# A hybrid of state-space scan, attention and routed experts on one core: the tail of the last image re-ordered

## The chip, the cores and the metric

The kernel runs on one core of a Trainium2 chip. The metric is device time in microseconds for one execution over four images. A core has TensorE (PE; its weight loads are listed as PEld), VectorE (DVE), ScalarE (ACT), GpSimd (POOL) and SyncE (SP). Each has its own queue and works through it in order. An engine waits when what stands at the head of its queue needs a result of another engine or of a transfer. Most transfers are issued from SP; the indirect ones, which scatter or gather rows by a list of places, from POOL.

## The reference, cut to what matters

The input x is 4 images of 384 channels by 32 by 32 positions, that is 1024 tokens per image.

```
# layer 0
x = x + gelu(layernorm(four-direction selective scan of groupnorm(x)))
# layer 1, on tokens t of width 384
t = t + softmax_causal(ln(t) Wq (ln(t) Wk)^T / sqrt(384)) ln(t) Wv
s = softmax(ln(t) gate_w + gate_b)             # 4 experts
keep the 2 largest of s per token, divide them by their sum + 1e-9
t = t + sum over the 2 kept e of s[e] * (gelu(ln(t) w1[e] + b1[e]) w2[e] + b2[e])
```

The selective scan of layer 0 runs over 1024 positions in four directions, for 384 channels with 16 states each. A hidden layer of an expert is 1536 wide. All is float32.

## The kernel before, in words

**Scan and ticks.** The scan is cut into 768 units (NU), 192 per image, each a 128 by 1024 tile. A loop over a counter called `clock` emits the program: in each tick it emits one unit of the scan (L192 decay, L648 input, L654 scan, L671 product, L696 row sums), and then as much other work as fits. The other work is written as Python generators. A generator yields ("pe", n) after n microseconds' worth of TensorE work, ("wait", k) to be taken up k ticks later, or ("inner", 0) to be taken up inside the next tick. `go_on` (L1837) hands out a budget per tick, `pace[0]`: 4.4 in attention (PACE_A), 3.1 elsewhere (PACE_E). Side generators get up to 1.0 each, and the first generator in `waiting` gets what is left. `defer(k, f)` puts an action k ticks later: mostly the copy that empties an accumulator. None of this is time on the chip; it only fixes the order in each engine's queue. From tick 772 (NU + 4) on there are no more scan units: what is emitted then is the tail.

**Buffers.** TensorE writes into banks of the accumulator memory. Four are free for side work in the scan; in the tail four more come (y_end and v_end, two halves each), eight in all. `banks.take` takes the one that has been free longest. Eight `slots` in on-chip memory are shared by weight tiles, blocks of rows and their results.

**The last image's layer.** After the scan of image b, `finish` does its layernorm (`layernorm`, L726): mean products (L739), subtraction (L747), squares on ACT, variance products (L766), square root on ACT, reciprocal (L779), products that spread the result over partitions (L785), multiplication (L795); then GELU on ACT, a load of x (xr, L971) and the addition (L979). `attention` follows: `scaled_tokens` does a second norm in the same manner (var_at L1000, L1011, L1015, L1020, L1036), then query products (pq, L1068), value products (pv, L1079), and for each of eight blocks of 128 tokens: scores (L1098), softmax on DVE and ACT, transposition (L1141), values (L1165, L1169), statistics (L1177). For images 0 to 2 this runs under the scan of the next image; for image 3 (`alone`) nothing is left to run under.

**Routing.** `ready` (L1220) routes the tokens in three groups, blocks 0 to 3, 4 and 5, 6 and 7: normalise, transpose (pxt, L1248), gate products (L1265), softmax with an exponential on ACT (L1284 to L1296), a comparison that counts the larger scores (L1297 to L1307), running counts (L1309), products that turn counts into places (L1324 to L1337), kept shares (mk, L1343 to L1347), places (L1355 to L1370), a transposition of mk (pm, L1376), and two scatters per block into xsd (L1385), which is in order of expert. After group 2, `table` (L1411) computes for each of NBLK = 11 blocks of 256 rows its expert, its place, and how many rows it holds.

**Experts.** `experts` (L1458) does the eleven blocks: load rows (xg, L1521), transpose (L1530), first product (ph, L1591) with GELU on ACT, second product (py, L1636), copy to yt (one half on DVE, L1650, one on ACT, L1652), store to ysd (L1654). Weight tiles are loaded (L1497) as slots come free. For the last image, six tiles go at a time, and a block computes 256, 128 or no rows, by its count: TensorE reads all eleven counts into registers (L1558) before the first block, and VectorE sets every accumulator to zero first (L1584, L1627), so that what isn't computed is zero.

**Combination.** For each block i of 128 tokens: gather the two expert rows of every token (L1682), load the token rows t2 and the gates (L1689, L1690), multiply identities by the shares on ACT, and sum on TensorE t2, b2 and the two choices (`add_up`, L1708); copy (L1715) and store (L1716). For image 2 this is `combine` and `joined`, which fall into the tail, around the last image's norms. For image 3, `early` is started when block 9 has been stored: first gathers, loads, and sums of all but the second choice; `late`, after block 10, gathers the second choice and ends the sums. The store of block 10 writes the tensor that the first gathers read, so it waits for them:

```
elif j == NBLK - 1:
    side.append((late if alone else combine)(b))
```

Of the kernel before, what the change touches and what calls it, by code (L numbers as in the profile page):

```python
# [9 lines left out]
F32 = mybir.dt.float32  # L10
# [7 lines left out]
P = 128  # L18
# [29 lines left out]
PACE_E = 3.1  # L48
BT = 256
# [6 lines left out]
def hybrid_kernel(  # L56
# [669 lines left out]
    def layernorm(dst, src, name, lag):  # L726
# [55 lines left out]
        for h in range(n):  # L782
# [8 lines left out]
            yield "pe", 1.0  # L791
        yield "inner", 0
# [193 lines left out]
    def scaled_tokens(b, yb):  # L986
# [19 lines left out]
        slots.give(*[f"sq_at_{b}_{c}" for c in range(M)])  # L1006
        rs = one.tile([P, NH, P], F32, tag=f"rs{NH}", name=f"rs_at_{b}")
# [212 lines left out]
    def ready(b, h, yb, rows, moments):  # L1220
# [42 lines left out]
        for q in range(n):  # L1263
            for c in range(M):
                nc.tensor.matmul(  # L1265
                    pg[:, q * E : (q + 1) * E], xts[q][:, c * P : (c + 1) * P], gw[:, c, :],
                    start=(c == 0), stop=(c == M - 1),
                )
        yield "pe", 0.65 * n
# [10 lines left out]
        def over(v):  # L1280
# [3 lines left out]
        nc.vector.tensor_reduce(red, sc, AX.X, ALU.max)  # L1284
        nc.vector.tensor_tensor(sc, sc, over(red), ALU.subtract)
        act(sc, sc, AF.Exp)

        cmp = [
            one.tile([P, 4, E, E], F32, tag=f"cmp{i}", name=f"cmp{i}_{name}")[:, :n] for i in range(2)
        ]  # L1290
        each = sc.unsqueeze(3).to_broadcast([P, n, E, E])
        other = sc.unsqueeze(2).to_broadcast([P, n, E, E])
        yield "wait", 1
        nc.vector.tensor_reduce(red, sc, AX.X, ALU.add)
        nc.vector.reciprocal(red, red)
        nc.vector.tensor_tensor(sc, sc, over(red), ALU.mult)  # L1296
        nc.vector.tensor_tensor(cmp[0], other, each, ALU.is_gt)  # L1297
        nc.vector.tensor_tensor(cmp[1], other, each, ALU.is_ge)
        nc.vector.tensor_tensor(
            cmp[1], cmp[1], lower.unsqueeze(1).to_broadcast([P, n, E, E]), ALU.mult  # L1300
        )
        nc.vector.tensor_tensor(cmp[0], cmp[0], cmp[1], ALU.max)
        cnt = small("cnt", name, n, E)
        nc.vector.tensor_reduce(cnt, cmp[0], AX.X, ALU.add)

        sel = small("sel", name, E, n)
        nc.vector.tensor_single_scalar(sel.rearrange("p e q -> p q e"), cnt, 1.5, ALU.is_lt)  # L1307
        cum = counts[b, h] = sm.tile([P, E, n], F32, tag=f"cum{h}", name=f"cum_{name}")
        nc.vector.tensor_tensor_scan(  # L1309
            cum.rearrange("p e q -> p (e q)"), fresh[n].rearrange("p e q -> p (e q)"),  # L1310
            sel.rearrange("p e q -> p (e q)"), 0.0, op0=ALU.mult, op1=ALU.add,
        )
# [22 lines left out]
        if h == LAST:  # L1335
            for i in range(LAST + 1):
# [3 lines left out]
                )  # L1340
        yield "pe", 1.5
        mk = small("mk", name, n, E)
        nc.vector.scalar_tensor_tensor(mk, cnt, 1.5, sc, ALU.is_lt, ALU.mult)  # L1343
        nc.vector.tensor_reduce(red, mk, AX.X, ALU.add)
        nc.vector.tensor_scalar_add(red, red, 1e-9)
        nc.vector.reciprocal(red, red)
        nc.vector.tensor_tensor(mk, mk, over(red), ALU.mult)  # L1347
# [25 lines left out]
        banks.give(f"place_{name}")  # L1373
        pm = yield from banks.take(f"pm_{name}")
# [7 lines left out]
        placed = places[b]  # L1382
        for q in range(n):
            for i in range(2):
                nc.gpsimd.indirect_dma_start(  # L1385
                    out=views[2 * (q0 + q) + i],
                    out_offset=bass.IndirectOffsetOnAxis(
                        ap=placed[:, q0 + q, i : i + 1], axis=0
                    ),
                    in_=rows[:, q, :], in_offset=None,  # L1390
                )
# [562 lines left out]
```

## Time and profile before

| | |
|---|---|
| Median of 3 runs | 3745.76 us (3745.48 to 3747.65) |
| Profiled execution | 3738.39 us |
| Its span, first to last instruction | 3736.7 us |
| Mean granted TensorE clock | 0.859 |
| PE busy | 2996.1 us (80%) |
| DVE busy | 3020.3 us (81%) |
| ACT busy | 2061.5 us (55%) |
| POOL busy | 1980.5 us (53%) |
| Moved by DMA | 798.42 MB, 214 GB/s over the span |

The last scan instruction ends at 3158.0 us, so the tail is 579 us long. A busy share is an average over the scan, where VectorE is at work nearly all the time, and the tail, where TensorE is. In the lines shown below, "out<-in" names what an instruction writes and reads, L and a number give its line, and the arrow in a line on waiting points to the engine, or the transfer, whose work came last.

### The profile page before, as it was taken

How to read it: one execution, taken by the hardware profiler on the slowest of the kernel's cores; microseconds unless marked ns; L12 is line 12 of the kernel's file. 1: busy time of each engine (PE TensorE's matmuls, PEld its weight loads, DVE VectorE, ACT ScalarE, POOL GpSimd, SP SyncE). 2: the span in 40 equal slices, each digit the busy share in tenths (PEclk: the TensorE clock that was granted, in tenths of full speed). 3: DMA queues.
4: the chain of work that ended last, by engine and by line, in shares of the span. 5: the costliest groups of instructions: out<-in, count | busy, mean ns of one | idle time of the engine just before them, and what ended most of it. 6: DMA issues, size and time to landing. Idle time of an engine off the chain costs nothing. (4 is left out here: it accounts for less than half of the span.)

```text
span 3736.7 us, 41646 instructions
## 1 busy us (share of the span) xinstructions
PE 2996.1 (80%) x13267; PEld 1798.4 (48%) x13267; DVE 3020.3 (81%) x2417; ACT 2061.5 (55%) x3268; POOL 1980.5 (53%) x931
## 2 busy tenths in 40 slices
PE   4566755678589899779569999779589999778997
PEld 1233423334346566344345665344256665556775
DVE  6999888899989999998999999999989998131110
ACT  5778787556466566456546665356356564342121
POOL 2677667645656555764656555765666666010001
PEclk7677777779789999769779999879689999888998
DMA  6658644543577888554567888553378876215555
GB/s 198 216 201 291 241 179 186 201 166 135 195 243 277 293 300 297 198 196 153 177 224 277 292 286 292 193 206 129 123 253 301 294 279 207 76 47 180 180 187 178
DMA packets 405202, 798.42 MB, mean 214 GB/s; under 512 B 47500, under 2 KB 278620, under 8 KB 404972
## 3 DMA queue, kind: packets, MB, share of 16 engines
q1 hardware_dynamic: 390572, 770.01, 59.3%
q0 software_dynamic: 8192, 25.17, 2.1%
q8 instruction: 117, 1.92, 0.2%
q10 hardware_dynamic: 6208, 0.39, 0.1%
q14 instruction: 113, 0.93, 0.1%
HBM read 680.44 MB, written 115.02 MB: 213 GB/s over the span
## 5 line engine op out<-in xcount | busy, mean ns | idle before, releaser
L671 POOL TENSOR_TENSOR h<-h,bc 128x1024 f32<-128x1024 f32 x768 | 1818.4, 2372 | 1208.9 <-DVE v L648 1031.8
L654 DVE TENSOR_TENSOR_SCAN h<-da,v 128x1024 f32<-128x1024 f32 x768 | 1749.3, 2283 | 80.7 <-PE v L958 40.8
L192 ACT ACTIVATE da<-dt,a 128x1024 f32<-128x1024 f32 x768 | 884.7, 1162 | 774.8 <-DVE h L654 636.7
L648 DVE TENSOR_TENSOR v<-du,bc 128x1024 f32<-128x1024 f32 x664 | 851.4, 1282 | 95.9 <-PE y L696 26.2
L696 PE MATMUL y<-h,sel 128*32 128x512 f32 x3072 | 560.0, 703 | 186.2 <-POOL h L671 178.6
L1591 PE MATMUL ph<-turned,w 128*128 128x256 f32 (+1 forms) x2772 | 631.1, 384 | 45.4 <-DMA w<-in_w 32.2
L1636 PE MATMUL py<-w,ht 128*128 128x384 f32 x1776 | 606.2, 493 | 11.3 <-DMA w<-in_w 11.3
L1591 PEld LDWEIGHTS ph<-turned,w 128*128 128x128 f32 x2772 | 523.4, 193 | 164.2 <-issue 51.1
L1636 PEld LDWEIGHTS py<-w,ht 128*128 128x128 f32 x1776 | 335.2, 192 | 277.7 <-issue 40.0
L192 ACT ACTIVATE ht<-ph,b1t 128x256 f32<-128x256 f32 x470 | 196.7, 471 | 330.6 <-PE ph L1591 329.8
L696 PEld LDWEIGHTS y<-h,sel 128*32 128x32 f32 x3072 | 104.4, 120 | 507.7 <-POOL h L671 290.6
L1682 POOL DMA_INDIRECT g<-ysd,places x64 | 83.4, 1303 | 369.6 <-DMA g<-gtd 329.8
L958 PE MATMUL v<-ident,st 128*128 128x128 f32 x832 | 156.5, 351 | 117.4 <-DVE h L654 113.0
L192 ACT ACTIVATE st<-turn,bt 128x128 f32<-128x128 f32 x832 | 245.4, 564 | 0.1
L958 PEld LDWEIGHTS v<-ident,st 128*128 128x128 f32 x832 | 127.7, 183 | 164.0 <-DVE h L654 94.6
L182 ACT ACT_TABLE_LOAD x122 | 156.5, 1283 | 12.2 <-issue 10.1
L510 PE MATMUL pdt<-xd,wdt 12*128 12x512 f32 x184 | 117.2, 774 | 23.5 <-ACT st L192 7.2
L1385 POOL DMA_INDIRECT xsd<-fx,places x32 | 36.3, 1135 | 153.6 <-DVE places L1370 145.8
L1169 PE MATMUL po<-vt,pt 128*128 128x384 f32 x242 | 91.6, 528 | 9.0 <-ACT pt L1059 9.0
L1098 PE MATMUL ss<-axn,qt 128*128 128x512 f32 (+3 forms) x252 | 91.8, 508 | 5.6 <-ACT pr L192 4.5
L192 ACT ACTIVATE dt<-pdt,dtb 128x512 f32<-128x512 f32 x96 | 64.6, 690 | 49.4 <-PE pdt L510 48.1
L192 ACT ACTIVATE ht<-ht 128x3072 f32<-128x3072 f32 x33 | 91.3, 2766 | 0.4
(381 smaller groups left out, 2656.1 us busy)
## 6 DMA issues: line engine op xcount, KB each, us to landing
w<-in_w SPq DMA_DIRECT2D x528, 384.0 KB
bc<-rows SPq DMA_DIRECT2D x384, 512.0 KB
dt<-dts SPq DMA_DIRECT2D x192, 512.0 KB
du<-dts SPq DMA_DIRECT2D x192, 512.0 KB
dts<-dt SPq DMA_DIRECT2D x48, 512.0 KB
dts<-du SPq DMA_DIRECT2D x48, 512.0 KB
xg<-xsd SPq DMA_DIRECT2D x44, 384.0 KB
ysd<-yt SPq DMA_DIRECT2D x44, 384.0 KB
```

Of the source, the lines that this page charges most:

```text
L182: nc.scalar.preload_act_table_set(kind)
L192: return nc.scalar.activation(dst, src, f, **more)
L510: nc.tensor.matmul(pss[i], wdt[r, m * P : (m + 1) * P], xd[r, bass.ts(h, 512)], start=True, stop=True,)
L648: return nc.vector.tensor_tensor(u["v"], spread["du4", n], spread["bc", n][:, 0, :], ALU.mult)
L654: nc.vector.tensor_tensor_scan(u["h"][:, ::step], u["da"][:, ::step], u["v"][:, ::step], 0.0, op0=ALU.mult, op1=ALU.add,)
L671: product = units[n]["product"] = nc.gpsimd.tensor_tensor(h, h, spread["bc", n][:, 1, :], ALU.mult)
L696: units[n]["row"] = nc.tensor.matmul(y, sel, h, start=first, stop=last, tile_position=(0, jj * DJ))
L958: nc.tensor.transpose(u["v"][:, t * P : (t + 1) * P], st[:, t, u["j"] * P : (u["j"] + 1) * P], ident)
L1098: nc.tensor.matmul(ps[:, : e - o], qt[:, c, i * P : (i + 1) * P], xn[o // 512][:, c, : e - o], start=(c == 0), stop=(c == M - 1 and (alone ...
L1169: nc.tensor.matmul(po[:, :C], pts[i][:, j, :], vt[:, j, :], start=False, stop=(j == i))
L1591: nc.tensor.matmul(ps[:, i * BT : i * BT + n], t[:, c, i * P : (i + 1) * P], xt[:, c, :n], start=(c == 0), stop=(c == M - 1),)
L1636: nc.tensor.matmul(pss[i][:, :C], hts[j][:, 2 * c + f, i * P : (i + 1) * P], tiles["2", j, c][0][:, f, :], start=(c == 0 and f == 0), stop ...
```

## The change

It does the following.

- **Finer steps.** From tick NU + 4 on the pace is 1.5 (PACE_T) in place of 4.4 or 3.1.
- **The third image's sums between the last image's norms.** `combine` is replaced for image 2 by `held_back`. It loads and gathers at the end of the scan into tiles that the scan leaves (not slots), and puts the eight sums on a list. `fill_in` takes from it: three sums after the spreading products of the last image's layernorm, two after the variance products of `scaled_tokens`, the remaining three after the gate products of group 2.
- **Experts by raw scores.** For the last image the comparison reads the scores, not the probabilities, which have the same order. The exponential, the probabilities and the kept shares come later: the scatters no longer stand behind the transposition of mk.
- **Registers and loads ahead.** TensorE reads the eleven counts when the first load of rows has been emitted, ahead of the transposes. Expert 0 is given at least one block, so that the first block's expert and place are known constants, in all images. Four weight tiles of the last image are loaded before routing ends.
- **Zeroing.** VectorE's zeroing is gone. Where a block has 128 rows or none, TensorE writes an identity over the rest, as a transpose: finite values, in rows that belong to no token and that no later step uses. This adds one branch.
- **The end.** t2 and gates of the last image are loaded when block 2 has been stored. The first choice is added to t2 by VectorE (`add_choice`); TensorE sums t2 and b2 of all eight blocks in eight banks (`sum_up`), and then only the second choice. The last block's copies are both on ACT.

The diff, cut to its core:

```diff
+PACE_T = 1.5
+PART = 2.6
...
             backs.append(spread_)
             yield "pe", 1.0
+        if name == f"l0_{B - 1}":
+            fill_in(3)
...
         slots.give(*[f"sq_at_{b}_{c}" for c in range(M)])
+        if b == B - 1:
+            fill_in(2)
...
+        if h == LAST:
+            gated.add((b, h))
...
+        if not alone:
+            exponents()
+            yield "wait", 1
+            probabilities()
+        cum = choice()
...
+        if alone:
+            exponents()
         yield "pe", 1.5
+        if not alone:
+            kept()
...
+        if alone:
+            yield "wait", 1
+            for q in range(n):
+                scatter(q)
+            routed.add((b, h))
+            probabilities()
+            kept()
+            yield "wait", 1
...
+        nc.vector.tensor_scalar_max(n, n, 1.0)
...
         def look_up(j):
+            if j == 0:
+                expert[j] = block[j] = 0
...
+        def by_rows(j, run, fill):
             with tc.If(filled[j] > P) as whole:
                 run(BT)
             with whole.Else():
-                with tc.If(filled[j] > 0):
+                fill(P)
+                with tc.If(filled[j] > 0) as some:
                     run(P)
+                with some.Else():
+                    fill(0)
...
-                    if alone:
-                        nc.vector.memset(ps, 0.0)
...
+                def fill(o):
+                    for f, t, w, name, ps in parts:
+                        for i in range(2):
+                            nc.tensor.transpose(
+                                ps[:, i * BT + o : i * BT + o + P], ident, ident
+                            )
...
-                        if alone:
-                            nc.vector.memset(pss[i][:, :C], 0.0)
...
+                def fill(o):
+                    if c0 == 0:
+                        for m in range(M):
+                            nc.tensor.transpose(pss[o // P][:, bass.ts(m, P)], ident, ident)
...
-                    if alone and i == 1:
+                    if alone and i == 1 and j < NBLK - 1:
...
-                if alone and j == NBLK - 2:
-                    side.append(early(b))
+                if alone and j == 2:
+                    side.append(beside_all(b))
+                elif alone and j == NBLK - 2:
+                    side.append(first_choice(b))
                 elif j == NBLK - 1:
-                    side.append((late if alone else combine)(b))
+                    side.append((late if alone else combine if b < B - 2 else held_back)(b))
...
+        while alone and fetched[0] < 4:
+            while not slots.ready():
+                yield "wait", 1
+            weights()
         while (b, LAST) not in routed:
             yield "wait", 1
         yield from load(0)
+        for j in range(NBLK if alone else 0):
+            count_rows(j)
...
+    def beside_all(b):
+        for i in range(L // P):
+            g = dtp.tile([P, L], F32, tag=("dt4", "du4")[i // 4], name=f"g_{b}_{i}")
+            z = (hp if i < 7 else dap).tile(
+                [P, L], F32, tag="h" if i < 7 else "da", name=f"z_{b}_{i}"
+            )
+            closing[b, i] = g, z
+            nc.sync.dma_start(z[:, :C], t2_d[b][bass.ts(i, P), :])
+            nc.sync.dma_start(g[:E, 2 * C : 2 * C + P], gates_d[b][:, bass.ts(i, P)])
+            for k in range(2) if b < B - 1 else (1,):
+                act(z[:, 2 * C + k * P : 2 * C + (k + 1) * P], ident, AF.Copy,
+                    scale=shares[b][:, i, k : k + 1])
+            yield "wait", 1
...
+    def held_back(b):
+        while clock[0] < NU:
+            yield "wait", 1
+        side.append(beside_all(b))
+        for i in range(L // P):
+            while (b, i) not in closing:
+                yield "wait", 1
+            g, z = closing[b, i]
+            for k in range(2):
+                gather(b, i, g, k)
+            ready_sums.append((b, i))
+            yield "wait", 1
+        while (B - 1, LAST) not in gated:
+            yield "wait", 1
+        while ready_sums:
+            fill_in(1)
+            yield "pe", 2.4
+
+    def fill_in(n):
+        for _ in range(min(n, len(ready_sums))):
+            b, i = ready_sums.pop(0)
+            g, z = closing[b, i]
+            ps = banks.now(f"pz_{b}_{i}")
+            add_up(ps, g, z, ("t2", "b2", 0, 1), True, True)
+            def put(b=b, i=i, ps=ps, z=z):
+                put_out(b, i, ps, z)
+                banks.give(f"pz_{b}_{i}")
+            defer(1, put)
+
+    def first_choice(b):
+        for i in range(L // P):
+            gather(b, i, closing[b, i][0], 0)
+        yield "wait", 2
+        for i in range(L // P):
+            add_choice(b, i, 0)
...
     def late(b):
...
+            gather(b, i, closing[b, i][0], 1)
+        pss = {}
         for i in range(L // P):
-            while len(closing[i]) < 3:
-                yield "wait", 1
-            g, z, ps = closing[i]
-            add_up(ps, g, z, (1,), False, True)
-            put_out(b, i, ps, z)
+            pss[i] = yield from banks.take(f"pz_{b}_{i}")
+            sum_up(b, i, pss[i], False)
+        for i in range(L // P):
+            g, z = closing[b, i]
+            for m in range(M):
+                nc.tensor.matmul(
+                    pss[i][:, bass.ts(m, P)], g[:, C + m * P : C + (m + 1) * P],
+                    z[:, 2 * C + P : 2 * C + 2 * P], start=False, stop=(m == M - 1),
+                )
+            put_out(b, i, pss[i], z)
...
     def go_on():
+        if clock[0] >= NU + 4:
+            pace[0] = PACE_T
```

## The prediction

> **What bounds the kernel now.** I read the page first: busy shares, the forty slices, then the chain. The scan loop of the first 3158 us is VectorE's; the change touches it only by one small VectorE operation per image (0.2 us each, three times) and fewer lookups on SP. So I went to the last 579 us.
>
> ```profile
> PE   4566755678589899779569999779589999778997
> ...
> DVE  6999888899989999998999999999989998131110
> ...
> PEclk7677777779789999769779999879689999888998
> ```
>
> Each digit is 93 us. In the last six VectorE is nearly idle, TensorE dips and recovers, and its clock with it. The table of stretches says where:
>
> ```profile
> 3200.00:3220.00 20.00, 12.70 (x147) 10.98 (x145) 2.27 (x3) 7.20 (x13) 0.00 (x0) 0.71 0.43 137
> 3360.00:3380.00 20.00, 4.40 (x13) 3.52 (x14) 4.34 (x20) 2.14 (x3) 2.98 (x4) 0.50 0.71 215
> 3440.00:3460.00 20.00, 20.00 (x73) 13.55 (x72) 0.83 (x2) 1.56 (x4) 0.00 (x0) 1.00 0.60 194
> ```
>
> (start:end, length, then PE, PEld, DVE, ACT, POOL busy, clock, DMA.) The norms and the routing leave TensorE waiting at a low clock; the experts fill it. The waits of 3333 to 3378, TensorE's alone, and of 3377 to 3690 name the latecomers:
>
> ```profile
> PE y_end L1530 <- DMA xg<-xsd: 11.2, 1, 11.2
> PE ph L1591 <- issue: 6.7, 1, 6.7
> ...
> PE v_end L1636 <- DMA w<-in_w: 7.6, 1, 7.6
> ...
> PE ph L1591 <- DVE ph L1584: 2.0, 1, 2.0
> PE v_end L1636 <- DVE v_end L1627: 1.9, 1, 1.9
> ```
>
> The end, in the chain:
>
> ```profile
> 3704.36 3.96 DMA g<-ysd,places
> ...
> 3708.87 2.51 DMA ysd<-yt
> ...
> 3718.41 4.29 DMA g<-ysd,places
> ...
> 3722.75 6.66 PE pz L1708 x30
> 3729.41 3.60 PE y_end L1708 x24
> ```
>
> The write of the last block waits for the first gathers, the second gathers for that write, and then ten microseconds of sums remain.
>
> **What the Trainium skill says.** "TensorE: Matmul & The Clock Gate", What's actually happening: an idle window of about 3.4 us halves TensorE's clock, a busy one restores it. The trace agrees in kind: after 7.6 us idle the pairs at L1636 take 1.62 us, 0.81 from 5.5 us later on. "ScalarE: Activation LUTs", What ACT_TABLE_LOAD costs: 1283 ns and a drain of 1380 after it. The trace has the 1283; the drain it doesn't show (load at 3301.12, next activation at 3302.42). "DMA: Bandwidth & Descriptors", Anatomy of one DMA — SWDGE (gpsimd) path: about 2.0 us fixed per DMA issued from GpSimd, plus bytes over 436 GB/s, which for a gather of 192 KB is an estimate of 2.45. The trace has 3.02 between POOL's end of the eighth gather and its landing, and 3.96 with POOL's own 0.94; I use the trace.
>
> **The change, part by part.** Letters mark stretches of the tail; times are those of the profile before, or worked out on its scale.
>
> A: norms, from the scan's last row product to the first query product; before 3164.0 to 3228.4.
> - Before, the squares (L192) start at 3175.9, though their input is there at 3168.6: ScalarE stands behind copies of the third image's sums. With these sums held back they start at 3168.6 and end at 3172.8. Six scalings (1.9), table 1.28, root 0.5, reciprocal 1.75, spread (L785) 3.5: 3181.9, against 3188.0.
> - Now three sums follow on TensorE, 3.25 each (0.83+0.93+1.60 less overlap): 3191.7. The GELU is behind their copies on ScalarE: 0.9+1.28+3.5 gives 3197.1 (before 3200.5). SP has the three output stores ahead of the xr loads, so these go at about 3193; the last needs 3.9 after issue as at 3200.52, and the adds (1.2 each) end near 3199.9, against 3205.7. So this place costs part of what it frees.
> - Squares 1.06 and variance 1.2: 3202.2. Two more sums, part of them at low clock (6.5 to 9.4; I take 8.4), then copy 0.5, table 1.28, root 0.5, reciprocal 1.75, spread 3.8: 3218.4. Gain 10 (6 to 14).
>
> B, C: projections and attention, 3228.4 to 3332.8. The matmuls are the same; a shorter pace makes the scheduler put copies and routing after fewer of them, and TensorE's own sequence keeps its order. Rows of groups 0 and 1 are now routed between scores and values: gates 2.6 twice, places 1.0, transposes 0.8+0.85 come ahead of the last value product, 7.9. The first place (L1324) follows its gate at once and waits for eight VectorE operations, 1.9. Idle time ahead of TensorE was 10.7 here; with more banks free I take 6 in its stead. Loss 5 (0 to 12).
>
> D: routing of group 2, counted from the last value product. Before: place matmuls end at +24.3, first expert product at +44.2.
> - Raw scores take reduce, subtract, exponential and four more steps off the choice (3351.35 to 3354.3 becomes 1.9). But VectorE has group 1's probabilities ahead of group 2's statistics (4 us), rows are ready at +8.5, gate ends at +12.6, and then the three held sums stand between gate and place on TensorE: 11, part of them cold, against a choice ready at +14.5. Place ends at +26.8.
> - From there four scatters, xg and transposes as before (3357.2 to 3370.9: 13.7), and the eleven count loads of 6.7 us run while xg is under way: tables are ready 4.9 after place, loads end at 11.6, xg lands at 11.7. So +40.8: gain 3.4 (-3 to 8). If xg came earlier, the loads would be late next.
>
> E: experts, 311 us. The zeroing on VectorE goes: 2.0+1.9+0.7 = 4.6 off. Fills on TensorE come: blocks 2 and 7 hold at most 128 rows (128x128 forms in the trace), 15 transposes each at 0.11: 3.3 on. Block 10 is empty; 30 fills, the first 12 ahead of a copy that SP's weight queue waits for: 1.3 on, the rest inside the 7.6 us weight wait. The t2 and gate loads move to block 2: six pairs, 0.92 each, stand on SP ahead of block 3's second weights, which are issued 6.4 before use; with the landing of 3.44 that is 2.7 on. Four weight tiles ahead of routing: their cover is that TensorE does not wait for weights at the first product anyway; nothing. The first block is known to be expert 0, so SP looks up one less in each image: nothing, since SP then waits for the scatters in any case. Keeping the count of blocks at one or more is the one VectorE operation counted below. Loss 2.5 (-4 to 6).
>
> F: from the last full product, X = 3688.5; before X+48.2. Loads of z and gates are gone from here, with the 2.1 hole behind the first gather. Gathers at X+4.7, 1.26 apart, last landed at X+17.5; block 10's write 0.55+2.5; second gathers from X+21.3, last landed X+34.4. VectorE adds choice 0 (0.5 each, between). TensorE's eight sums of t2 and b2 start at X+9.5 cold: five at 3.27, three at 1.76, X+31; eight last terms of 0.77: X+37; copy 0.5, store 3.2: X+40.6. Gain 7.6 (1 to 10; 1 if cold throughout).
>
> Sixteen scalings of 0.3 on ScalarE leave this stretch too; they stood between the copies of blocks 9 and 10, and block 10's write waited for the gathers anyway: nothing.
>
> Sum: 10-5+3.4-2.5+7.6 = 13.5, less 0.5 for VectorE's three operations in the scan loop: 13. Span 3736.7 becomes 3723.7, its execution 3738.4 becomes 3725.4. The median shown, 3745.8, lies 7.4 above that execution, for which the page gives no reason; I take the difference over: 3733.
>
> **The rivals.**
> - Smaller: TensorE stays cold where sums are bunched. D's three at 6 each add 7, F's tail cold adds 4 to 6: 13-12 = 1, so 3745. For it: clock 0.50 at 3340 to 3380, 0.77 at the end. Against: each bunch is itself activity, and 5.5 us of it sufficed at 3669.9.
> - Larger: attention has none of the 6 us of waits that I left it, and the weight wait of 7.6 shrinks by 4, since VectorE no longer copies yt among its zeroing: 13+10 = 23, 3723. For: the waits there are all for ScalarE's copies or exponentials, which hold a bank or the next operand. Against: ScalarE does the same work, with routing's operations now between.
> - Slower: SP's weight queue falls one tile behind at block 2 and does not recover. Price: one tile's landing, 3.44, in nine blocks is 31, less the 2.7 counted: -13+28 = +15, 3761. It decides once the nine lose 2.6 each: 13+2.7+7.5 over nine. For: ysd writes wait behind ScalarE copies, weights behind them. Against: SP waited 53+38+31 us for TensorE in this stage, so it has room to catch up.
> - The raw-score choice does nothing: that is in the forecast, since in D the sums hide it.
>
> **How the numbers follow.** Forecast 0.48, smaller 0.22, larger 0.22, slower 0.08. About 0.2% (7.5 us) is what can be told from no change. Forecast and larger are faster; of smaller a third is; the rest of it is the same: 0.77, 0.15, 0.08. Bounds of A to F taken together give some 10 either way about 3733; the larger case with A's upper bound is the lower end, the smaller case the upper: 3719 to 3745. The forecast's own range is 3726 to 3739.
>
> **What would show it.** First query product 8 to 12 earlier; GELU right behind three copies; value loads of TensorE ahead of the xg transposes, and the first expert product about 9 earlier; no zeroing on VectorE; a weight wait of some 3 us in block 3; the end 40 us behind the last full product. Wrong it would be if TensorE waited for in_w in several blocks, or if the place of group 2 came over 30 us behind the last value product.

## The result and the profile after

| | before | after |
|---|---|---|
| Median of 9 runs | 3744.17 us | 3732.76 us |
| Range | 3734.58 to 3747.65 | 3729.08 to 3738.2 |
| Profiled execution | 3738.39 us | 3731.26 us |
| Its span | 3736.7 us | 3729.6 us |

The ratio is 0.9977, 95% interval 0.9968 to 0.9986: faster by 0.23%, little more than what can be told from no change. The forecast was 3733. The total fell where it was put, but its stages did not.

The table takes both traces apart by the letters of the prediction: each number is the distance between two instructions on TensorE, counted from the end of the last row sums (3164.03 before, 3166.08 after). A third column is the changed kernel run once more, to show how far such distances repeat.

| stage | before | after | again | gain, after | predicted |
|---|---|---|---|---|---|
| A norms | 64.4 | 57.3 | 58.7 | 7.1 | 10 |
| B, C projections and attention | 104.5 | 108.9 | 107.7 | -4.4 | -5 |
| D routing of group 2 | 44.2 | 43.2 | 42.9 | 1.0 | 3.4 |
| E experts | 311.4 | 307.5 | 308.1 | 3.9 | -2.5 |
| F end | 48.2 | 46.7 | 46.3 | 1.5 | 7.6 |
| tail, A to F | 572.7 | 563.5 | 563.6 | 9.2 | 13.5 |

Between these two traces the tail repeats to 0.1, single stages to 1.4. Over the traces below in which the code of a stage is unchanged the spread is wider: A 57.3 to 60.1 (and some 65 on one chip, see Norms), B and C 105.9 to 108.9, D 40.1 to 43.2, E 307.3 to 308.1, F 45.1 to 47.5. The kernel before has one trace, so the gains of 1.0 in D and 1.5 in F lie within that spread. The scan before the tail repeats less well: its end lay between 3161 and 3184 in the traces made here. So the stages are compared, not the spans; single runs of the whole kernel differ by that much without any cause in the tail.

The slices of the profile after (each digit is 93 us):

```profile
PE   4566756678589999769669998869679999788998
...
DVE  6999888899989999998999998999999999220000
...
PEclk7677777779789999779779999879689999889997
```

VectorE, whose last digits were 131110, is now idle in the experts. The last clock digit fell from 8 to 7. The table of stretches of the kernel after (start:end, length, PE, PEld, DVE, ACT, POOL busy, clock, DMA):

```profile
3200.00:3220.00 20.00, 13.34 (x154) 11.43 (x155) 6.02 (x6) 6.30 (x8) 0.00 (x0) 0.76 0.31 113
...
3360.00:3380.00 20.00, 6.70 (x30) 5.56 (x30) 6.08 (x42) 2.38 (x4) 3.83 (x4) 0.66 0.38 126
3440.00:3460.00 20.00, 20.00 (x81) 14.60 (x80) 0.42 (x1) 3.31 (x8) 0.00 (x0) 1.00 0.42 131
3690.00:3710.00 20.00, 18.37 (x70) 15.86 (x71) 4.95 (x8) 0.00 (x0) 10.83 (x11) 0.50 0.40 119
```

The norms and the routing still leave TensorE idle. New is the last line: 18.4 of 20 us busy, and at half clock all the time. Waits of TensorE, in routing and then in the experts:

```profile
PE pm L1421 <- issue: 13.1, 1, 13.1
PE pxt L1254 <- ACT rows L194: 3.6, 1, 3.6
...
PE v_end L1683 <- DMA w<-in_w: 5.9, 3, 4.7
PE y_end L1683 <- DMA w<-in_w: 1.7, 1, 1.7
PE y_end L1571 <- ACT ht L194: 1.0, 2, 0.5
PE v_end L1571 <- ACT ht L194: 0.5, 1, 0.5
```

The waits for zeroing (2.0, 1.9, 0.7) are gone. The 13.1 holds the eleven value loads. The 1.7 is the weight wait of block 3 that was forecast as 3, the 4.7 the one of block 10 that was 7.6. The chain at the end:

```profile
3690.58 3.48 DMA g<-ysd,places
...
3694.86 1.62 PE pz L1839 x6
3696.47 1.57 PE pz L1842 x6
...
3715.39 1.57 PE y_end L1842 x6
3716.97 2.86 PE pz L1903 x12
```

Before, the chain went through first gathers, store and second gathers. Now it is TensorE's sums from 3694.9 on, each group of six at 1.6: all eight sums cold.

### The profile page after: what moved, and what is told of

It reads as the page before. It is cut to its first block, busy times and chain, and to the rows that moved or that the text cites. A ratio compares the mean times of both kernels' runs of the same rounds, so it can differ in the third digit from the quotient of the medians.

```text
span 3729.6 us, 41269 instructions
## 1 busy us (share of the span) xinstructions
PE 2995.7 (80%) x13279; PEld 1790.8 (48%) x13279; DVE 2984.6 (80%) x2340; ACT 2057.4 (55%) x3261; POOL 1979.5 (53%) x931
## 4 chain that ended last, share of the span: by engine, by line
PE 30%; DVE 26%; DMA 6%; issue 2%; ACT 2%; SPq 1%; POOL 1%; DVEq 0%; ACTq 0%; POOLq 0%
DVE h L656 14%; DVE v L650 8%; PE ph L1633 8%; PE py L1683 7%; DMA w<-in_w 3%; PE y L698 2%; PE v_end L1683 2%; PE y_end L1683 1%; PE pq L1074 1%; PE pv L1085 1%; DMA du<-dts 1%; PE y_end L1633 1%; PE ss L1104 1%; POOL h L673 1%; PE v_end L1633 1%
## 5 line engine op out<-in xcount | busy, mean ns | idle before, releaser
L1633 PEld LDWEIGHTS ph<-turned,w 128*128 128x128 f32 x2784 | 522.2, 192 | 152.8 <-issue 45.5
L1683 PE MATMUL py<-w,ht 128*128 128x384 f32 x1704 | 579.7, 493 | 13.2 <-DMA w<-in_w 13.2
L1683 PEld LDWEIGHTS py<-w,ht 128*128 128x128 f32 x1704 | 320.5, 191 | 269.7 <-issue 43.4
```

The lines of the kernel that those rows point to most:

```text
L1633: nc.tensor.matmul(ps[:, i * BT : i * BT + n], t[:, c, i * P : (i + 1) * P], xt[:, c, :n], start=(c == 0), stop=(c == M - 1),)
L1683: nc.tensor.matmul(pss[i][:, :C], hts[j][:, 2 * c + f, i * P : (i + 1) * P], tiles["2", j, c][0][:, f, :], start=(c == 0 and f == 0), stop ...
```

## The experiments

The first four kernels of the table shared a chip, then the fixed banks, norms, routing and warm, then the last three and the repeat. Stage times, from one profiled execution each (so mind the spread given above):

| kernel | A | B, C | D | E | F | tail |
|---|---|---|---|---|---|---|
| zeroing back | 60.1 | 107.7 | 42.9 | 318.3 | 46.4 | 575.5 |
| old end | 57.8 | 105.9 | 40.1 | 305.5 | 48.6 | 557.8 |
| sums at once | 63.8 | 110.3 | 32.8 | 321.6 | 45.1 | 573.6 |
| pace 3.1 | 57.5 | 94.7 | 45.5 | 317.0 | 46.0 | 560.7 |
| fixed banks | 64.8 | 94.6 | 48.7 | 297.4 | 48.7 | 554.0 |
| norms | 53.5 | 106.0 | 40.7 | 309.2 | 45.4 | 554.9 |
| routing | 64.7 | 109.0 | 36.2 | 315.9 | 46.3 | 572.1 |
| warm | 66.4 | 107.4 | 43.1 | 307.5 | 41.4 | 565.9 |
| registers | 60.1 | 107.5 | 47.0 | 307.3 | 46.0 | 568.0 |
| probabilities | 57.6 | 102.1 | 41.5 | 311.1 | 47.5 | 559.8 |
| combination | 50.7 | 96.7 | 48.7 | 298.3 | 44.1 | 538.5 |

**Zeroing back.**

```diff
-                fill(P)
-                with tc.If(filled[j] > 0) as some:
+                with tc.If(filled[j] > 0):
                     run(P)
-                with some.Else():
-                    fill(0)
...
                     ps = yield from banks.take(name)
+                    if alone:
+                        nc.vector.memset(ps, 0.0)
...
                         pss[i] = yield from banks.take(f"py_{b}_{j}_{i}")
+                        if alone:
+                            nc.vector.memset(pss[i][:, :C], 0.0)
```

> The last image's experts zero their PSUM banks on VectorE again, as before; the transposes that take the zeroing's place are gone, and the branch for an empty block with them. The rest is as in the changed kernel. Read in E (first expert product to the last full product; 307.5 us in the changed kernel). My prediction's sum (4.6 of zeroing off, 4.6 of transposes on) says E 307.5 again, within 1. The theory from the two traces (the zeroing stops TensorE at a moment that also leaves its clock at half for the next dozen products): the waits of 4.6 come back, twice 1.8 of low clock come back, 3.3 of transposes on the path go: E 312.4, 311 to 314. A third, that the gain of E came from somewhere else (the moved loads of t2 and gates): E 304 to 308. A, B/C, D and F unchanged within 1.5 in all three.

E was 318.3, 10.8 longer: more than any theory had. The timeline of VectorE and TensorE there (start, length, then the instruction and in brackets the idle time before it):

```profile
3466.84 0.56 DVE L1703 COPY yt<-v_end 128x384 f32<-128x384 f32 x1 [27.29 <-ACT yt L1705]
3467.51 0.48 DVE L1625 MEMSET ph<- 128x512 f32 x1
...
3468.09 2.83 PE L1632 MATMUL ph<-turned,w 128*128 128x256 f32 x12 [1.87 <-issue]
...
3620.99 4.51 PE L1632 MATMUL ph<-turned,w 128*128 128x256 f32 x12 [1.88 <-issue]
```

The zeroing stands behind the copy of yt in VectorE's queue, and that copy behind ScalarE's. So TensorE waits here not for 0.48 of zeroing but for two copies on two engines. It does so in three places of E (1.9, 1.2 and 1.9); in four more it waits 0.8 for zeroing with no copy just ahead. Of the two long waits one left TensorE at half clock, twelve products taking 4.51; after the other they took 2.83. By the free list every accumulator of E is in the same bank as in the changed kernel, so the order of banks, told of below, plays no part in the 10.8.

TensorE's waits in E, added up from the traces (gaps of over 0.15; those named issue count as zeroing, the rest of "all" is for ScalarE):

| | for zeroing | for weights | all | not waiting |
|---|---|---|---|---|
| before | 5.4 | 7.6 | 15.6 | 295.8 |
| after | 0 | 7.6 | 9.4 | 298.0 |
| zeroing back | 8.0 | 11.5 | 21.0 | 297.3 |

So undoing it costs 8.0 of waits for zeroing and 3.9 more for weights; the transposes that are gone (6.6 in the trace) and the longer time of the products at a lower clock nearly cancel. Undone in the changed kernel, the zeroing is the dearest part of the change in E, and the prediction had it at nothing. In the kernel before it stalled TensorE less.

**Old end.** The functions `early` and `late` as in the kernel before; started behind block 9 and block 10.

```diff
-                if alone and j == 2:
-                    side.append(beside_all(b))
-                elif alone and j == NBLK - 2:
-                    side.append(first_choice(b))
+                if alone and j == NBLK - 2:
+                    side.append(early(b))
...
```

> The end of the last image as before: t2 and gates loaded behind the first gathers, the scalings on ScalarE, sums of t2, b2 and choice 0 on TensorE while the second gathers run; the copies of the last block stay on ScalarE. The rest is as in the changed kernel. Read in F (last full product to the end; 46.7 us changed, 48.2 before) and in E (307.5). Theory 1, the prediction's: the new end is worth 7.6, F 54. Theory 2, from the traces: TensorE stays at half clock through the sums in both forms, so the new end is worth what was measured between the two kernels, 1.5: F 48 to 49. In E theory 1 has the moved loads cost 2.7 at block 3, so E 304.8 here; theory 2, since only one wait of 1.72 for a weight is left there, E 305.5 to 306.5. If E stays at 307.5, the wait in block 3 is not due to those loads.

F 48.6, E 305.5: theory 2 in both. The new end is worth 1.9 (1.1 to 3.5 over the traces with an unchanged F), and its loads, moved to block 2, cost 1.8 to 2.6 in E; the wait of 1.7 for a weight in block 3 is gone in this trace. Together they are worth nothing that these traces can tell. The tail is 5.7 shorter all the same, by B, C and D, whose code is unchanged: TensorE waits there for 27.7, against 27.6 in the changed kernel, but its clock was higher (0.95 and 0.67 in the two stages, against 0.92 and 0.62).

**Warm.**

```diff
             gather(b, i, closing[b, i][0], 0)
+        warm = banks.now(f"warm_{b}")
+        for n in range(72):
+            nc.tensor.transpose(warm[:, n % 4 * P : (n % 4 + 1) * P], ident, ident)
+        banks.give(f"warm_{b}")
```

> The changed kernel with 72 transposes of the identity into an unused bank, whose results nobody reads, on TensorE behind the first gathers of the last image, that is in the wait ahead of the last eight sums. Read in F (46.7) and in the time of one group of three fp32 128x128 matmuls in the eight sums (1.65 at half clock, 0.84 at full). Theory 1: the half clock of the sums comes from the idle time ahead of them; kept busy, TensorE does the eight sums in 14 rather than 26, and F is 4 to 8 shorter, bound by the second gathers then: F 39 to 43. Theory 2: the sums stay at half clock whatever stands ahead (the power of the chip, or the kind of matmul): F 46 to 48. Theory 3: sums go fast, but the gathers and the last stores end F: F 45 to 47 with sums of 0.84.

The stretches of this kernel that hold the sums:

```profile
3690.00:3710.00 20.00, 18.84 (x132) 15.91 (x131) 3.71 (x6) 1.34 (x3) 6.84 (x8) 1.00 0.40 120
3710.00:3730.00 20.00, 15.91 (x101) 13.72 (x100) 1.86 (x3) 2.91 (x7) 8.39 (x9) 0.91 0.58 168
```

Theory 1: the clock is 1.00 where it was 0.50, a group of six takes 0.94, and F falls by 5.2 to 41.4. The chain is back at the first gathers, the store of block 10 and the second gathers, so the rest of the sums' gain (26 to 15) is hidden behind those. The waiting ahead of the sums, 7.6 us, had left the clock at half.

**Sums at once.**

```diff
-side.append((late if alone else combine if b < B - 2 else held_back)(b))
+side.append((late if alone else combine)(b))
```

> The third image's sums are no longer held back: they are gathered and summed as soon as its experts are done, as before. The rest is as in the changed kernel. Read in A (row sums' end to first query product; 57.3 changed, 64.4 before) and in D (last value product to first expert product; 43.2 changed, 44.2 before). Theory 1: the sums between the norms gain in A what the comparison shows, 7, and the three sums left for the routing cost D what they take on TensorE between gate and place, so that A is 64 and D 43.2 less some 11 (place is ready at +14.5 from the last value product rather than +28): D 30 to 34, and the whole is 4 shorter than the changed kernel, though holding back was meant to gain. Theory 2, the prediction's chain (past the place the count loads of TensorE and the landing of xg set D): place earlier, loads earlier too, D follows in full, the same 30 to 34. Rival: D is bound by something else (scatters on POOL behind the gathers, statistics on VectorE), and D stays at 40 to 43, the whole 4 to 7 longer.

In A and D theory 1 holds: A 63.8, D 32.8 with the place at +17.8. Holding the sums back gains 6.5 in A and loses 10.4 in D (3.7 to 6.5 and 7.3 to 10.4 over the traces). But the tail was 10 longer, not 4 shorter, since E was 321.6, 14.1 longer. No theory had that. In E the instructions of TensorE and VectorE stand in the same order in both kernels, those of SP but for one branch, those of ScalarE but for how some copies of the transposes are joined. What differs is which accumulator bank each product gets: the free list was left in another order, and only 29 of the 110 accumulators of E are in the same bank. Waits make up 9 of the 14, a lower clock the rest (0.973 in E, against 0.987). The longest waits in E:

```profile
PE y_end L1683 <- DMA w<-in_w: 4.3, 1, 4.3
PE py L1683 <- DMA w<-in_w: 3.8, 1, 3.8
PE y_end L1641 <- ACT yt L1704: 3.6, 3, 2.2
PE v_end L1571 <- ACT yt L1704: 2.8, 1, 2.8
```

Those for yt are new; those for weights add up to 8.1, hardly more than the 7.6 of the changed kernel. The longest for yt in the timeline, ScalarE and TensorE:

```profile
3645.75 0.51 ACT L1704 COPY yt<-v_end 128x384 f32<-128x384 f32 x1
...
3646.31 0.66 PE L1571 MATMUL v_end<-ident,xg 128*128 128x128 f32 x4 [2.81 <-ACT yt L1704]
```

By the free list the transposes write bank 6 here, and the copy reads bank 7: the other half of v_end. The wait ends as that copy ends. Bank 6 itself was emptied a block earlier. The other waits for yt go the same way (banks 5 and 4 of y_end).

**Fixed banks.** To test it, the pace of the next experiment and

```diff
+    def own_bank(name):
+        what, *n = name.split("_")
+        if what not in ("ph", "py", "pxg") or int(n[0]) < B - 1:
+            return None
+        if what == "ph":
+            return (4, 5, 0, 6, 7, 1)[int(n[2]) // 2]
+        return 2 + (int(n[2]) if what == "py" else int(n[2]) // 2)
...
-                    if alone and i == 1 and j < NBLK - 1:
+                    if alone and j < NBLK - 1:
```

> The changed kernel with pace 3.1 in the tail, and with the PSUM banks of the last image's experts fixed by hand: first products in banks 4, 5, 0 and 6, 7, 1, second products and transposes in banks 2 and 3; VectorE copies both halves of yt, except the last block's. (Banks 4, 5 are the halves of one tile, y_end; 6, 7 of v_end.) With pace 3.1 alone E was 317.0, 9.5 longer than in the changed kernel, with TensorE's instructions in the same order. Theory of banks: which bank the free list hands out decides which copy a product must wait for, and a write to one half of a wide tile also waits for the reader of the other half; with fixed banks the waits for ht and yt (11 in E with pace 3.1) are gone, and with them some low clock: E 304 to 308, B/C and D as with pace 3.1 alone (94.7 and 45.5, within 2). Rival: the waits follow from the pace, that is from when copies are queued on ScalarE: E stays at 314 to 318. A second rival: without these waits TensorE runs into the weights: waits for w grow by as much, E 312 to 318.

```profile
PE py L1699 <- DMA w<-in_w: 3.0, 1, 3.0
PE y_end L1649 <- ACT turned L1593: 0.2, 1, 0.2
```

These are all of TensorE's waits in E, 3.2 us, where pace 3.1 alone had 16 us. E is 297.4, 19.6 shorter and below the range I gave: the waits for weights fell too, from 5.0 to 3.0, and the clock rose (0.994 in E, against 0.978). What is shown is the worth of the banks together with VectorE's copying of yt; the two were not run apart, so how much of it is the banks' stays open. (A is longer by a stall told of below. B, C is 94.6, as with pace 3.1 alone; D, 48.7, is 3.2 longer, more than the 2 allowed for, with the place 2.4 later.)

**Pace 3.1.**

```diff
-        if clock[0] >= NU + 4:
-            pace[0] = PACE_T
```

> The scheduler's pace stays at 3.1 in the tail, rather than 1.5. The rest is as in the changed kernel. Read in B/C (first query product to the last value product; 108.9 changed, 104.5 before) and D (43.2). Theory 1: the finer pace brings the routing of groups 0 and 1 ahead of the last value product, which costs 4.4 in B/C and saves it in D: here B/C 104 to 106, D 45 to 48, the sum of both unchanged within 2. Theory 2: the pace also took waits away in the projections: B/C 108 to 113 and D 45 to 48, the sum 3 to 8 longer. Rival: the order of routing against attention is set by the waits for banks and copies, not by the pace: both stages unchanged within 1.

B, C 94.7 and D 45.5: together 140.2 against 152.1 (150.6 in the repeat, 146.0 in the lowest trace of the finer pace). The rival that the pace does nothing falls, and so do both theories: the finer pace took no waits away, it cost 6 to 12 here. Ahead of the last value product it puts routing whose gates and places TensorE then waits for; the waits are 5 of it (22 against 27 to 28 in the traces of the finer pace), a lower clock the rest, which differs among those traces too. E was longer by 9.5, with new waits (transposes waiting for ht, twice 1.7, and others for yt) that fixed banks remove, which made the sum look neutral.

**Probabilities.** The choice as before, by probabilities:

```diff
-        if not alone:
-            exponents()
-            yield "wait", 1
-            probabilities()
+        exponents()
+        yield "wait", 1
+        probabilities()
         cum = choice()
```

> The changed kernel, but the last image's experts are chosen by probabilities, as before: maximum, subtraction, exponential, sum, reciprocal and product ahead of the choice, the shares ahead of the scatters. Read in D and B/C. The prediction: in group 2 the three held sums (15 on TensorE) cover the longer choice: D unchanged within 1.5 (40 to 44.5). Rival: places of groups 0 and 1 come later, rows wait for them, and D or B/C is 3 to 6 longer in sum (B/C plus D 152.1 in the first trace, 146 to 152 over the runs).

D 41.5, in the range of the prediction: the sums hide the longer choice. But B, C is 102.1, and with D 143.6 against 150.6 beside it on the chip. The choice by raw scores loses 7 there, 2 to 9 against all traces (146.0 to 152.1). The waits show 3 of it, the clock the rest. Without the step of the scheduler that the exponential brought, the place products of group 0 follow their gates at once (wait 1.7), and the transposes of group 1's shares wait 2.6 for shares that are computed later; with it, a value product stands between.

**Registers.**

```diff
-        for j in range(NBLK if alone else 0):
-            count_rows(j)
...
+            if not filled:
+                for n in range(NBLK):
+                    count_rows(n)
```

> The changed kernel, but TensorE loads the eleven row counts at its first expert product, as before, rather than while it waits for xg. Read in D (43.2 in the first trace; 40 to 43.5 over the runs with the same code there). The prediction: the loads, 6.7, come behind the transposes of xg and in front of the first product: D 46.5 to 50. Rival: in the changed kernel the loads end last, behind the table, and not xg: then most of the 6.7 is paid in either form, D 43 to 45.

TensorE's timeline of this kernel, in which the place ends at 3365.4:

```profile
3376.65 1.52 PE L1571 MATMUL pxg<-ident,xg 128*128 128x128 f32 x6 [4.33 <-DMA xg<-xsd]
3384.72 4.53 PE L1636 MATMUL v_end<-turned,w 128*128 128x256 f32 x12 [6.55 <-issue]
```

D 47.0, 4.1 longer than the repeat: the prediction's 46.5 to 50. Here xg is ready 11.3 after the place; in the changed kernel its transposes come at 13.4, behind the loads. So of the 6.7 some 2 are still paid.

**Norms.**

```diff
-        if name == f"l0_{B - 1}":
-            fill_in(3)
         yield "inner", 0
...
             banks.give(f"rb_{name}_{h}")
+        if name == f"l0_{B - 1}":
+            fill_in(3, 3)
...
-            fill_in(2)
+            fill_in(2, 4)
...
```

(The second number is the ticks by which copy and store are put off.)

> The changed kernel, but in A the three sums are issued behind the first norm's last multiplication, and their copies and stores three scheduler steps later; the copies of the two sums of the second norm four steps later. Read in A (57.3). Theory: in A the sums' copies stand on ScalarE ahead of the GELU, and their stores on SP ahead of the xr loads; without these the GELU starts 6 to 8 earlier, xr with it, and the square root right behind the variance: A 44 to 50. Rival: A is set by TensorE's own sums (five at 3.2 to 3.3 between norms that need it for 12 matmuls): A 54 to 58. The stages behind keep their order; E may shift by some us either way, because other banks come up: no theory on it.

A was 53.5, above the 44 to 50 of the theory. In this and the three kernels beside it on that chip the square root behind the first norm's variance came 7.0 to 7.5 later (19.2 to 19.4 behind the row sums, against 11.9 to 12.2 in the other traces of the change that hold the sums back). Part of that, 3 and more, lies among the last variance products, in gaps of 0.3 to 1.8 for which the trace shows nothing to wait for. Against its neighbours with the same A as the changed kernel (64.7, 64.8, 66.4) it is 11 to 13 shorter, but they stall too: in the combination below, which has no stall, A is 7 to 9 shorter than beside it. ScalarE now has the GELU and the squares ahead of the copies:

```profile
3201.36 3.50 ACT L194 ACTIVATE yb<-yb,lnb,lnw 128x1024 f32<-128x1024 f32 x3 [6.21 <-DVE yb L797]
3204.77 2.93 ACT L194 ACTIVATE sq_at<-yb 128x1024 f32<-128x1024 f32 x3
3207.61 0.46 ACT L1775 COPY z<-y_end 128x384 f32<-128x384 f32 x1
```

**Routing.**

```diff
-        if h == LAST:
-            gated.add((b, h))
...
+            gated.add((b, h))
+        if alone and h > 0:
+            fill_in(1)
...
+        if alone and h == 1:
+            fill_in(1)
```

> The changed kernel, but the last three of the third image's sums are issued one behind the place matmuls of group 1, one behind the transposes of its shares, one behind the place matmuls of group 2, rather than all three between gate and place of group 2. Read in D (43.2). Theory 1 (the prediction's D: sums of 15 between gate and place set it; without sums at all D was 32.8, place at +17.8): D 32 to 37, place at +16 to +22. Theory 2: TensorE's value loads and the landing of xg set D whatever the place does: D 40 to 43. B/C unchanged within 3.

Place at +20.7, D 36.2: theory 1; B, C is unchanged at 109.0. The whole lost it again in E (315.9: five waits for yt, 0.9 to 2.1).

**Again** (no edit).

> The changed kernel once more, unaltered, on the chip of the three others. It tells how far the stages repeat. If the stall of 7 in A (variance products that wait for nothing in the trace) belongs to the chip and the session, A is 64 to 66 here if the others of this call have it, and 57 if they have not. If it belongs to where a kernel's instructions lie, A is 57 as at first, whatever the others show. B/C 105 to 109, D 40 to 43.5, E 306 to 309, F 45.5 to 47.

A 58.7 and no stall, as with the others on its chip: the stall belongs to the four runs on the one chip, not to the program. Whether to the chip or to the hour is open. The other stages are within the ranges.

**Combination:** pace 3.1, fixed banks, norms, routing and warm.

> Together: pace 3.1 in the tail, fixed banks for the last experts with VectorE copying yt, the later copies in A, the spread-out sums in D, the 72 transposes ahead of the last sums. If the single gains add (A 11 shorter, B/C and D 12 to 18 shorter by pace and sums, E 10 shorter, F 5 shorter than the changed kernel), the tail from the row sums' end is 515 to 528 rather than 563.5, 7 more where TensorE stalls in the first variance products as it did in the four runs before these, and the kernel takes 3690 to 3702, 0.988 to 0.990 of the kernel before. Rival: what one stage gives the next takes back (earlier routing waits for weights, earlier experts for SP): 3710 to 3725, 0.992 to 0.996.

Median 3704.4 (3701.55 to 3707.21); ratio to the kernel before 0.9896, interval 0.9874 to 0.9919. It beats both kernels: the kernel before, beside it on the chip, by 40, and the changed kernel's median by 28. The tail is 538.5 against 563.6; 515 to 528 was expected, and 3690 to 3702 for the whole. So neither the sum of the single gains nor the rival was met. E 9.8 and A 8.0 came; B, C and D together came to 145.4, no better than pace 3.1 alone with its 140.2, the place being at +32.4; F is 44.1, not 41.4. That the spread-out sums fit the finer pace and not this one would explain it, but was not run apart.

## Why the prediction was right, and where it was not

The total was right by luck, because misses cancelled: four stages fell short of their numbers by 11 together (A 2.9, D 2.4, F 6.1, less 0.6 in B, C), E was 6.4 better. The tail gained 9.2 of the 13.5 forecast. The executions profiled differ by 7.1, the medians by 11.4; the scan's own spread covers that.

Of the signs that it named, counted from the end of the row sums, the first query product came 7.1 earlier (8 to 12 forecast), the first expert product 3.7 (9), and the end 46.7 behind the last full product (40). The order of copies and value loads, the missing zeroing and the wait in block 3 were as forecast. TensorE did wait for weights in several blocks, its sign of being wrong (0.6, 1.7, 0.6, 4.7), but for no longer in all than before (7.6).

- **A, 10 predicted, 7.1 measured.** Mechanism and order held: squares at +4.6, GELU behind three copies, out stores ahead of the xr loads. The last addition ended at +37.7 and not +35.9, and the variance products 3.4 behind it and not 2.3; the two sums took 6.4 and not 8.4. The sum also ends with the spreading products, and sets their end, 3218.4, against the first query product before: the multiplication between the two, 1.85, is missing. With it the forecast would have been 8.2.
- **B, C, -5 predicted, -4.4.** The size was right and its cause partly: routing between scores and values. That the pace and the choice by raw scores cost 6 to 12 and 2 to 9 (not additive), the prediction did not see; it took the latter for harmless because it looked at D alone.
- **D, 3.4 predicted, 1.0.** The step "the three held sums stand between gate and place" was right, its term too small: 15.1, not 11. The loads end 13.1 behind the place, not 11.6. The gain measured is within the spread.
- **E, -2.5 predicted, 3.9: the largest miss.** "4.6 off, 4.6 on" counted the waits that the trace named and put the transposes against them. What it left out is told by the table of waits above. A stall costs more than its own length: before, twelve products behind the wait of 2.0 took 4.51, not 2.83. The wait for weights at the end shrank from 7.6 to 4.7, which paid for the 1.7 that the moved loads brought in block 3 and two more waits of 0.6. The transposes took 6.6 in all, part of it inside that wait, much as the prediction had it. In all, waits fell by 6.2 and the time in which TensorE did not wait rose by 2.2. The 10.8 of the experiment is the price of the zeroing in the changed kernel, where it stalls TensorE for 8.0; before, it stalled it for 5.4. Only 41 of the 110 accumulators of E have the same bank in both, and bank order moved E by 14 at an unchanged order of TensorE's instructions; that this is why the two prices differ is likely but not shown, since the kernel before was not run with fixed banks.
- **F, 7.6 predicted, 1.5.** The bound "1 if cold throughout" was the case. The step "five at 3.27, three at 1.76" is what the sums of the kernel before did: they started at half clock and were back at full clock 17 us later.

```profile
3693.62 1.62 PE L1708 MATMUL y_end<-ident,z 128*128 128x128 f32 x6 [5.10 <-DMA z<-t2d]
...
3711.31 0.83 PE L1708 MATMUL v_end<-ident,z 128*128 128x128 f32 x6
```

After, all eight took 3.15 to 3.3: the clock stayed at half for 34 us, from 3687.2 on. The warm kernel shows the term: 5.2.

Of the rivals, the smaller one was right in its mechanism, bunched sums staying cold; the slower one (weights a tile behind in nine blocks) was not: three short waits and the 4.7. The larger one's weight wait did shrink, 7.6 to 4.7. Against the smaller one the prediction held that 5.5 us of activity had sufficed in the experts; the trace shows 6.2 there (3669.89 to 3676.10), and the sums needed far more.

"TensorE: Matmul & The Clock Gate" of the Trainium skill, What's actually happening, says that a busy window restores the clock. In the experts it came back so. The sums, 26 us at 0.50 and busy for 18.4 of 20, did not bring it back; transposes ahead of them kept it at 1.00.

## What to carry to other kernels

When buffers come from a free list, an edit elsewhere can reorder it, and the stage behind changes by more than the edit's own worth: compare stages, and fix the buffers of the long stage before judging small edits by the whole. Take a wait's price from undoing it, since the engine named may itself queue behind another; the price found so holds for the kernel in which it was undone. Repeat a trace before believing a stage to 2 or 3 us: at the same waits, the granted clock alone moved B to D by 6. Filler between dependent steps is worth only what it leaves free on every queue that its copies and stores pass.

## What the runs showed of the hardware

- After 7.6 us of waiting, TensorE did 26 us of 128x128 products, nearly without a gap, at half clock (1.65 for six). Before the change, after waiting 5.1, the same kind of sums came back after 17. In the experts, after waiting 4.7, 128x384 products were back at full clock 6.2 us later (3664.26 to 3670.48). What tells the three apart was not tried.
- A product into one half of a two-bank tile waited for a copy that reads the other half (2.81 us, ended 0.05 after the copy). Whether the chip asks for that wait or only this program does, no run tells.
- In four traces on one chip the square root behind 48 variance products came 7.0 to 7.5 us later than in the traces from two other chips with the same order of work, with gaps among the last products for which the trace names no cause.
